# Attention of the first batch in float32 in a cross-attention and FFN kernel, with its inputs on two queues and a new order

## The chip, the cores and the metric

The kernel runs on one core of a Trainium2 chip. The measure is device time in microseconds (us) of the slowest core, here the only one. Three runs of the kernel before took 427.7, 428.87 and 428.94 us; the median is 428.87.

The core has five engines that run side by side, each through its own list of instructions in order: TensorE (PE; the loading of its weights is shown apart, as PEld), VectorE (DVE), ScalarE (ACT), GpSimd (POOL) and SyncE (SP), which here does nothing but start transfers. Engines wait for each other by semaphores.

## The reference

The input `x` is 8 batches x 512 tokens x 512 columns, `ctx` 8 x 64 memory tokens x 512, and a mask says which memory tokens count. First comes attention over the memory tokens, then a feed-forward network (FFN) whose weights are rounded to three values and whose activations are rounded to 8 bits:

```python
def _L0_xattn_ref(hidden_states, memory_tokens, memory_mask):
    scale = 1.0 / jnp.sqrt(D)
    scores = jnp.einsum('bsd,bmd->bsm', hidden_states, memory_tokens) * scale
    scores = jnp.where(memory_mask[:, None, :], scores, -1e30)
    attn = jax.nn.softmax(scores, axis=-1)
    readout = jnp.einsum('bsm,bmd->bsd', attn, memory_tokens)
    valid_b = jnp.any(memory_mask, axis=-1)
    return jnp.where(valid_b[:, None, None], readout, 0)

def _rmsnorm(x, g):
    return g * (x * jax.lax.rsqrt(jnp.mean(x * x, axis=-1, keepdims=True) + EPS))

def _act_quant(x):
    scale = 127.0 / jnp.clip(jnp.max(jnp.abs(x), axis=-1, keepdims=True), 0.0001, None)
    return jnp.clip(jnp.round(x * scale), -128, 127) / scale

def _ternary_quant(w):
    s = jnp.mean(jnp.abs(w))
    return jnp.round(jnp.tanh(w / (s + EPS))) * jnp.arctanh(s)

def _linear_bit(x, w, g):
    return jnp.einsum('bsd,od->bso', _act_quant(_rmsnorm(x, g)), _ternary_quant(w))

x = x + _L0_xattn_ref(_layernorm(x), ctx, mask)
y = _layernorm(x)
h = _silu(_linear_bit(y, w1, g1)) * _linear_bit(y, w2, g2)
x = x + _linear_bit(h, w3, g3)
```

`w1` and `w2` are 2048 x 512, `w3` is 512 x 2048, all float32 (4 MB each). Before a weight can be rounded, the mean of all its magnitudes must be known, so all of it must have been read.

## The kernel before, in words

**The program and its order.** The kernel first records its program as a list of operations in a `Plan`: each has an engine, an estimated cost for the planner, the call that issues it, and the buffers that it reads and writes. Some have several `ways` (the same work on another engine). `ORDER`, a compressed string, holds the order in which all operations are issued and the way that each takes; it was written by a planner outside the program. `Plan.order` decodes it, gives each tile its place in its pool, and the program is issued in just that order:

```python
    order, ways = plan.order()
    with tc.manual_schedule():
        for o in order:
            plan.ops[o].ways[ways[o]][2]()
```

So each engine's list is fixed, and so is that of SP, which starts every transfer of the program: all inputs, all outputs and all transposes that a DMA makes (`Q` is SP). `A` is ACT, `V` DVE, `G` POOL, `T` PE. The cost numbers in the calls of `op` do not reach the chip.

**Tiles.** A batch is four tiles of 128 tokens (tile c of batch b; partition p holds tokens 4p to 4p+3). The 64 memory tokens of a batch lie twice, in partitions 0 to 63 and 64 to 127, in `mem_b`, loaded by two transfers of 128 KB (`load_x`, L469 to 487). `both_b` holds two batches' memory tokens for `measure_mem` (L489 to 526), which finds the power of two of each batch's largest magnitude and from it the scales `f`. Batch 0's x comes in two halves of 512 KB, other batches' in one of 1 MB.

**Attention.** It is done with float16 pairs: a float32 value is written as a high half (a cast to float16) plus a low half (the rest, cast again), and both go through float16 products.
- `split_mem` (L528) makes `ms`, the scaled memory tokens as a pair (high half on ACT L533, low half on DVE L536), and their transpose `mT`.
- `pre` (L542): statistics of x by DVE (L560, L562), the normalised tile `t` (L582, L586), its pair `xh` (L591, L592), its transpose `xT`, and scores `psc` (L602), eight products of 128x128 with k over the four 128-column blocks of both halves. Then two passes on DVE put scale, bias of the mask and the second half of the scores together (L614, L618), the maximum (L622) and the difference (L624).
- `expo` (L630): the exponential, on ACT (L645).
- `post` (L651): the sum and its inverse, times the scale in `f` (L663), the pair `ph` of the weights (high half, and L670 for the low half), its transpose `pT`, the readout `po` (L683, eight products of 128x512), and x plus the readout (L691).
- `flip` (L293 to 310) transposes a float16 tile: for batch 0 on PE, with a copy from PSUM to SBUF by DVE (L309) or ACT (L310); for other batches by a transpose in a DMA that SP starts.

Batch 0 goes through this in two halves, tiles 0 and 1, then 2 and 3. `masks` (L274 to 287) loads the mask (64 KB), and DVE makes `keep`, the bias and `valid` (which batches have any token) from it.

**The weights.** `load_w` (L316) reads each weight in four quarters, `raw_i_k`, of 1 MB. `measure_w` (L339 to 373) sums the magnitudes of each quarter, on ACT (L353) or DVE (L354), the last quarter in two halves; one product with a matrix of constants adds the partitions (`pm`, L363), and DVE makes the mean and the scale `ws` (L371). `quantise_w` (L380) then rounds each quarter: it scales to a float16 that rounds by its own spacing (`tq`, on POOL L386 or ACT L387, or DVE), transposes it on PE (`pw`, 16 transposes, L396) and clips it into `w1T`, `w2T` or `w3T` on DVE (L390 by its line). `arctanh` makes the factor `alpha`.

**The FFN.** `quantise_x` makes z for one or two tiles: the second layernorm (`xm`, L721, L725, L731), times g1 and g2 (`z`, L736 on POOL), the largest magnitude (L741), the rounding (L799, L800) and the transpose `zT`, on PE for batch 0 and by DMA for batches 1 to 7. For each tile, `gate` and `up` make `p` by `linear` (L883; a group is eight products of 128x512, four groups a tile), silu on ACT (L899), the product with it on DVE (`combine`, L927), squares on ACT (L932), g3 (`gain`, L940, on POOL or DVE), the largest magnitude (L964 by its line) and the rounding of h (L997 by ACT, or POOL); two transfers of a transpose make the halves of `hT` (L1002). `down_quarter` multiplies with `w3T` (`pd`, L825), four quarters of four products between the groups of a later tile, and DVE adds to x (L835). The last tile of all has its own order (`down_last`, L854).

During the FFN of batch b, the attention of batches b+1 and b+2 and the z of batch b+1 are worked on between the groups (`during`). For batch 0, the rounding of w3 stands there too. PSUM has three places of two banks that `p`, `pw`, `po` and the transposes of batch 0 share.

## Time and profile before

One execution was profiled. It took 427.9 us in all; the span of its instructions, from the first to the last, is 425.8 us.

| | busy us | share of the span | instructions |
|---|---|---|---|
| PE, products | 388.8 | 91% | 2174 |
| DVE | 369.0 | 87% | 832 |
| ACT | 341.3 | 80% | 464 |
| POOL | 368.7 | 87% | 330 |
| DMA, mean of the span | 67.35 MB at 158 GB/s | | |

The costliest groups of instructions:

| line, engine, work | count | busy us | mean ns of one |
|---|---|---|---|
| L883 PE, p from w1 | 512 | 120.4 | 383 |
| L883 PE, p from w2 | 512 | 119.2 | 379 |
| L825 PE, pd | 496 | 117.8 | 379 |
| L940 POOL, h times g3 | 55 | 130.4 | 2377 |
| L927 DVE, combine | 64 | 81.9 | 1280 |
| L964 DVE, largest of h, 2048 columns | 31 | 70.6 | 2278 |
| L899 ACT, silu | 64 | 70.1 | 1105 |
| L592 POOL, low half of x | 32 | 37.3 | 1168 |

A product's shown 380 ns is longer than the time by which the next follows it (16 products of 512 columns stand in the chain of waits with 3.46 us: 216 ns for one, 1.73 us for a group of eight), since products overlap.

Busy time is the union of an engine's instructions. In the views that follow, the slices cut the span in 40 equal parts of 10.6 us and give the busy share in tenths (9 is 90% or more); PEclk is the clock that TensorE was granted, in tenths. The chain of waits follows back from the last instruction to what released each; its lines give start, length and what ran. The timeline gives start, length, engine, line and operation, and in brackets how long the engine had been idle and for what.

Up to 40 us the transfers moved 13.87 MB, 347 GB/s in the mean. The mask (64 KB) landed 3.2 us after its issue, a half of batch 0's x 6.1 us, a `both` 8.7 us, a quarter of a weight 13.8 us (medians of the first 40 us). ACT's first instruction, the load of a table of 1.28 us, is followed by its first copy of memory tokens; it was idle 8.5 us for that. DVE's reduction of batch 0's `both` took 0.69 us.

### The profile page before, as it was taken

To read this page: it belongs to the slowest core of one execution; us is meant where nothing else is said; L and a number is where in the kernel's file an instruction comes from. 1 tells how busy PE (TensorE), PEld (TensorE's weight loads), DVE (VectorE), ACT (ScalarE), POOL (GpSimd) and SP (SyncE) were. 2 spreads that over 40 slices of the span, in tenths; PEclk is the share of its full clock that TensorE was granted. 3 is DMA by queue.
4 is the path that set the end of the run, shared out by engine and by line. 5 is a ranking of instruction groups with operands and counts; after the bars stand their busy time and mean duration, and the time that the engine had idled before them with its cause. 6 is when DMAs were issued, how large, how long until landed. Compare 5 with 4: busy or idle time off the path is not lost.

```text
span 425.8 us, 6677 instructions
## 1 busy us (share of the span) xinstructions
PE 388.8 (91%) x2174; PEld 192.8 (45%) x2174; DVE 369.0 (87%) x832; ACT 341.3 (80%) x464; POOL 368.7 (87%) x330
## 2 busy tenths in 40 slices
PE   0563878999999999999999999999999999999996
PEld 0341534544444544454445444544454444444444
DVE  4689999999998998799989998999789888897772
ACT  1799999979899799598996898988686986774531
POOL 1789998998999999699999999999699979988650
PEclk9996899999999999999999999999999999999999
DMA  7999994497555578863589635864644546533272
GB/s 217 408 406 376 380 208 52 103 255 147 126 112 150 99 131 157 183 174 68 104 158 276 136 76 82 171 174 83 134 76 148 75 87 146 152 77 73 49 207 90
DMA packets 142514, 67.35 MB, mean 158 GB/s; under 512 B 133136, under 2 KB 133520, under 8 KB 140048
## 3 DMA queue, kind: packets, MB, share of 16 engines
q1 hardware_dynamic: 142480, 66.93, 63.4%
q8 instruction: 17, 0.28, 0.3%
q14 instruction: 17, 0.14, 0.1%
HBM read 25.76 MB, written 8.39 MB: 80 GB/s over the span
## 4 chain that ended last, share of the span: by engine, by line
PE 78%; DVE 6%; POOL 6%; DMA 3%; issue 3%; ACT 2%; SPq 0%; DVEq 0%; POOLq 0%; ACTq 0%
PE p L883 48%; PE pd L825 24%; PE po L683 3%; DMA zT<-xm 2%; PE psc L602 2%; POOL tq L386 2%; DVE st L560 1%; DMA both<-in_ctx_dram 1%; PE pd L854 1%; POOL t L586 1%; POOL xh L592 1%; POOL mv L291 1%; DVE zf L741 1%; DVE h L927 1%; ACT h L899 1%
## 5 line engine op out<-in xcount | busy, mean ns | idle before, releaser
L883 PEld LDWEIGHTS <-zT 128*128 128x128 f16 x1024 | 99.5, 98 | 122.0 <-issue 3.0
L940 POOL TENSOR_TENSOR h<-h,g_bc 128x1024 f32<-128x1024 f32 x55 | 130.4, 2377 | 2.7 <-ACT sq L932 2.1
L883 PE MATMUL p<-w1T,zT 128*128 128x512 f16 x512 | 120.4, 383 | 2.4 <-DVE zT L309 1.5
L883 PE MATMUL p<-w2T,zT 128*128 128x512 f16 x512 | 119.2, 379 | 1.1 <-DVE h L927 0.9
L825 PE MATMUL pd<-w3T,hT 128*128 128x512 f16 x496 | 117.8, 379 | 0.0
L927 DVE SCALAR_TENSOR_TENSOR h<-p,zf,h 128x1024 f32<-128x1024 f32 x64 | 81.9, 1280 | 14.9 <-PE p L883 8.4
L899 ACT ACTIVATE h<-p,zf 128x1024 f32<-128x1024 f32 x64 | 70.1, 1105 | 24.8 <-PE p L883 17.0
L932 ACT ACTIVATE sq<-h 128x1024 f16<-128x1024 f32 x64 | 67.2, 1050 | 17.0 <-DVE h L927 14.8
L825 PEld LDWEIGHTS <-hT 128*128 128x128 f16 x496 | 47.9, 98 | 55.6 <-DMA hT<-h 0.2
L964 DVE TENSOR_REDUCE hf<-h 128x1 f32<-128x2048 f32 x31 | 70.6, 2278 | 1.8 <-POOL h L940 1.7
L736 POOL TENSOR_TENSOR z<-xm,g_bc 128x1024 f32<-128x1024 f32 x29 | 69.8, 2423 | 1.4 <-ACT xm L725 0.6
L997 ACT ACTIVATE h<-h,hf 128x2048 f16<-128x2048 f32 x23 | 45.8, 1994 | 0.2 <-DVE hf L968 0.2
L741 DVE TENSOR_REDUCE zf<-z 128x2 f32<-128x1024 f32 x32 | 38.8, 1211 | 5.8 <-POOL z L736 5.7
L592 POOL TENSOR_TENSOR xh<-t,xh 128x512 f16<-128x512 f32 x32 | 37.3, 1168 | 2.0 <-DVE xh L591 1.2
L799 ACT ACTIVATE xm<-z,zf 128x512 f16<-128x512 f32 x42 | 28.1, 709 | 0.7 <-DVE zf L760 0.7
L731 ACT ACTIVATE xsq<-x,xf 128x512 f32<-128x512 f32 x32 | 22.9, 715 | 6.5 <-DVE x L691 6.0
L835 DVE SCALAR_TENSOR_TENSOR x<-pd,hf,x 128x512 f32<-128x512 f32 x31 | 23.1, 744 | 3.0 <-PE pd L825 2.6
L691 DVE SCALAR_TENSOR_TENSOR x<-po,mx,x 128x512 f32<-128x512 f32 x32 | 22.9, 745 | 1.3 <-PE po L683 1.2
L602 PE MATMUL psc<-mT,xT 128*128 128x128 f16 x256 | 19.7, 224 | 1.9 <-DMA xT<-xh 1.9
L560 DVE BATCH_NORM_STATS2 st<-x 128x6 f32<-128x512 f32 x32 | 21.3, 679 | 0.0
L602 PEld LDWEIGHTS <-xT 128*128 128x128 f16 x256 | 16.9, 101 | 8.5 <-DMA xT<-xh 3.5
L291 POOL TENSOR_TENSOR hf<-hf,neg_half 128x1 f32<-128x1 f32 x32 | 20.1, 634 | 0.2
(134 smaller groups left out, 483.4 us busy)
## 6 DMA issues: line engine op xcount, KB each, us to landing
raw<-in_L_ffn_w_dram SPq DMA_DIRECT2D x10, 1024.0 KB, 13.8
x<-in_x_dram SPq DMA_DIRECT2D x7, 1024.0 KB, 6.9
out_dram<-x SPq DMA_DIRECT2D x7, 1024.0 KB, 4.1
mem<-in_ctx_dram SPq DMA_DIRECT2D x16, 128.0 KB, 6.5
w3T<-in_L_ffn_w_dram SPq DMA_DIRECT2D x2, 1024.0 KB, 12.6
both<-in_ctx_dram SPq DMA_DIRECT2D x4, 256.0 KB, 8.2
x<-in_x_dram SPq DMA_DIRECT2D x2, 512.0 KB, 6.1
g_bc<-in_L_ffn_g_dram SPq DMA_DIRECT2D x1, 1024.0 KB, 14.9
```

The lines of the kernel that those rows point to most:

```text
L592: rest = lambda e, t=t, xh=xh: e.tensor_tensor(xh()[:, 1, :], t(), xh()[:, 0, :], ALU.subtract)
L602: T.matmul(psc()[:, c, :, :].rearrange("p s m -> p (s m)"), xT()[:, k, :], mT().rearrange("p (s d) m -> p d s m", s=2)[:, k % ND, :, :], s ...
L736: gain = lambda e, xm=xm, z=z: e.tensor_tensor(z(), xm().broadcast_to([P, 2, D]), g_bc(), ALU.mult)
L741: lambda i=i, z=z, am=am: V.tensor_reduce(am()[:, i, :], z(), AX.X, ALU.max, apply_absolute_value=True),
L825: T.matmul(po(), hT()[:, n * P : (n + 1) * P], w3T()[:, n, :], start=(n == 0), stop=(n == NH - 1),)
L883: T.matmul(ps()[:, k * HC : (k + 1) * HC], zT()[:, g * ND + d, :], weight(d, j * HW // HC + k), start=(d == 0), stop=(d == ND - 1),)
L899: lambda: A.activation(h()[:, j * HW : (j + 1) * HW], ps(), AF.Silu, scale=fac()[:, 0:1]),
L927: lambda: V.scalar_tensor_tensor(cols(), ps(), fac()[:, 1:2], cols(), ALU.mult, ALU.mult),
L932: lambda: A.activation(sq(), cols(), AF.Square, scale=(RMS / H) ** 0.5, accum_out=col(j)),
L940: run = lambda e: e.tensor_tensor(cols(), cols(), g3_bc()[:, j * HW : (j + 1) * HW], ALU.mult)
L964: lambda: V.tensor_reduce(col(2), h(), AX.X, ALU.max, apply_absolute_value=True),
L997: op(ACT, 1995, lambda: A.activation(hq(), h(), AF.Copy, scale=col(5)), [h], [(f, 5)], other=[(POOL, 1970, lambda: G.tensor_scalar(hq(), h ...
```

## The change

- For the batches in `FLOAT`, here batch 0 alone, no pair is made. `turn_float` transposes the float32 tile on PE with the float32 identity, into a PSUM tile of float32, and copies it to SBUF on DVE or ACT; the buffers `mT`, `xT` and `pT` keep their places and are read as float32 by `as_float`. The scores are four float32 products of 128x64 for a tile in place of eight of 128x128 in float16, the readout one of 128x512 for a tile in place of two. One pass on DVE adds the bias, with the constant scale D^-0.5; the inverse of the sum is multiplied by `valid`; the readout is made with `mem` itself.
- The mask and `mem_0` go through ACT's queue, and the memory tokens of each batch come twice into their tile by one transfer with a broadcast source, not by two transfers. (`both_0` is still loaded, since batch 1 needs it.)
- `ORDER` is another. In it SP starts with the first half of x, then `both_0`, the second half of x, and w1's quarters 3, 1, 0, 2. DVE sums the magnitudes of two and a half quarters of w1 in place of ACT, DVE multiplies more tiles by g3, and the copies of batch 0's transposes are on ACT.
- A few costs for the planner change; they do not reach the chip.

```diff
--- before.py
+++ after.py
@@ -149,47 +150,47 @@
 
 
 ORDER = """
...
 """
 BIG, XM, BOTH = 9, 2, 1
 LAST = 1
+FLOAT = (0,)
 TURNED = ((0, 1, 2, 3), (0, 1, 2, 3), (0, 1, 2, 3))
 Z_TURNED = (0, 1, 2, 3)
 AHEAD = 0
@@ -272,8 +273,8 @@
         op(DVE, 140, lambda: V.tensor_copy(ident_h(), ident()), [ident_h], [ident])
 
     def masks():
-        op(DMA, (475, 650, 200, 500),
-           lambda: Q.dma_start(
+        op(DMA, (60, 650, 200, 500),
+           lambda: A.dma_start(
                mask_u8().rearrange("p b m -> p (b m)"),
                mask.rearrange("b m -> (b m)").partition_broadcast(P)),
            [mask_u8], [])
...
@@ -467,16 +468,18 @@
     xs, mts, att_state, mem_f = {}, {}, {}, {}
 
     def load_x(b):
-        if b % 2 == 0:
+        if b % 2 == 0 and not {b, b + 1} <= {*FLOAT}:
             both = plan.buffer(att, "both", [P, D], F32, BOTH, f"both_{b}")
             op(DMA, (475, 650, 729),
                lambda: Q.dma_start(both(), mem[b : b + 2].rearrange("b m d -> (b m) d")), [both], [])
             mem_f[b] = mem_f[b + 1] = measure_mem(b, both)
         mt = plan.buffer(att, "mem", [P, D], F32, 2, f"mem_{b}")
-        for half in range(2):
-            op(DMA, (475, 650, 364, 500),
-               lambda half=half: Q.dma_start(mt()[half * M : (half + 1) * M, :], mem[b]),
-               [(mt, half)], [])
+        queue = A if b == 0 else Q
+
+        op(DMA, (60 if b == 0 else 475, 650, 700, 500),
+           lambda: queue.dma_start(
+               mt(), mem[b : b + 1].broadcast_to([2, M, D])),
+           [(mt, 0), (mt, 1)], [])
         xt = plan.buffer(big, "big", [P, NC, D], F32, BIG, f"x_{b}")
         view = x[b].rearrange("(p c) d -> p c d", c=NC)
         n = 2 if b == 0 else NC
@@ -485,6 +488,10 @@
                lambda c=c: Q.dma_start(xt()[:, c : c + n, :], view[:, c : c + n, :]),
                [(xt, c + i) for i in range(n)], [])
         mts[b], xs[b] = mt, xt
+
+    def as_float(buf, n):
+
+        return buf().rearrange("p n r -> p (n r)").bitcast(F32).rearrange("p (n r) -> p n r", n=n)
 
     def measure_mem(b, both):
 
@@ -525,7 +532,24 @@
            [(f, 3)], [pe, valid])
         return f
 
+    def turn_float(name, buf, made, rows, n, src, reads):
+
+        pt = plan.buffer(ps_mm, "mm", [P, n, rows], F32, 3, f"pt_{name}")
+
+        def turn():
+            for i in range(n):
+                T.transpose(pt()[:, i, :], src()[:, i * P : (i + 1) * P], ident()[:rows, :rows])
+
+        op(PE4, 107 * n * rows // P, turn, [pt], [*reads, ident])
+        op(DVE, 151 + n * rows * 25 // 24, lambda: V.tensor_copy(made(), pt()), [buf], [pt],
+           other=[(ACT, 140 + n * rows * 5 // 6, lambda: A.copy(made(), pt()))])
+
     def split_mem(b):
+        if b in FLOAT:
+            mT = plan.buffer(att, "mT", [P, 2 * ND, M], F16, 2, f"mT_{b}")
+            turn_float(f"m_{b}", mT, lambda: as_float(mT, ND), M, ND, lambda: mts[b]()[0:M, :],
+                       [(mts[b], 0)])
+            return mts[b], mT, None
         mt, f = mts[b], mem_f[b]
         ms = plan.buffer(att, "ms", [P, 2, D], F16, 2, f"ms_{b}")
         mT = plan.buffer(att, "mT", [P, 2 * ND, M], F16, 2, f"mT_{b}")
@@ -586,6 +610,20 @@
                        lambda c=c, t=t, scale=scale, shift=shift, by=by: by.tensor_scalar(
                            t(), xt()[:, c, :], scale(), shift(), ALU.mult, ALU.add))
                       for e, by, cost in ((POOL, G, 762), (DVE2, V, 545))])
+            if b in FLOAT:
+                xT = plan.buffer(att, "xT", [P, 2 * ND, P], F16, 2, f"xT_{b}_{c}")
+                turn_float(f"x_{b}_{c}", xT, lambda xT=xT: as_float(xT, ND), P, ND, t, [t])
+
+                def score(c=c, xT=xT):
+                    for k in range(ND):
+                        T.matmul(
+                            psc()[:, c, 0, :], as_float(xT, ND)[:, k, :], as_float(mT, ND)[:, k, :],
+                            start=(k == 0), stop=(k == ND - 1),
+                        )
+
+                op(PE4, 860, score, [(psc, c)], [xT, mT])
+                yield
+                continue
             xh = plan.buffer(att, "xh", [P, 2, D], F16, 2, f"xh_{b}_{c}")
             op(ACT, 612, lambda t=t, xh=xh: A.copy(xh()[:, 0, :], t()), [(xh, 0)], [t],
                other=[(DVE2, 413, lambda t=t, xh=xh: V.tensor_copy(xh()[:, 0, :], t()))])
@@ -610,14 +648,17 @@
             yield
         bias_b = lambda: mask_bias()[:, b : b + 1, :].broadcast_to([P, n, M])
         part, cost = lambda: sc()[:, lo:hi, :], 139 + 67 * n
+        by = (lambda: float(D) ** -0.5) if b in FLOAT else (lambda: f()[:, 3 + b % 2 : 4 + b % 2])
+        scaled = [] if b in FLOAT else [(f, 2)]
         op(DVE, cost + 66,
            lambda: V.scalar_tensor_tensor(
-               part(), psc()[:, lo:hi, 0, :], f()[:, 3 + b % 2 : 4 + b % 2], bias_b(), ALU.mult, ALU.add),
-           [(sc, lo)], [*((psc, c) for c in tiles), (f, 2), mask_bias])
-        op(DVE, cost + 66,
-           lambda: V.scalar_tensor_tensor(
-               part(), psc()[:, lo:hi, 1, :], f()[:, 3 + b % 2 : 4 + b % 2], part(), ALU.mult, ALU.add),
-           [(sc, lo)], [*((psc, c) for c in tiles), (f, 2)])
+               part(), psc()[:, lo:hi, 0, :], by(), bias_b(), ALU.mult, ALU.add),
+           [(sc, lo)], [*((psc, c) for c in tiles), *scaled, mask_bias])
+        if b not in FLOAT:
+            op(DVE, cost + 66,
+               lambda: V.scalar_tensor_tensor(
+                   part(), psc()[:, lo:hi, 1, :], by(), part(), ALU.mult, ALU.add),
+               [(sc, lo)], [*((psc, c) for c in tiles), *scaled])
         top = lambda: mx()[:, lo:hi]
         op(DVE, cost, lambda: V.tensor_reduce(top(), part(), AX.X, ALU.max),
            [(mx, lo)], [(sc, lo)])
@@ -635,7 +676,7 @@
             for b in batches:
                 post_state[b] = (
                     plan.buffer(att, "pr", [P, NC, M], F32, 1, f"pr_{b}"),
-                    plan.buffer(att, "ph", [P, NC, 2, M], F16, 1, f"ph_{b}"),
+                    None if b in FLOAT else plan.buffer(att, "ph", [P, NC, 2, M], F16, 1, f"ph_{b}"),
                     plan.buffer(att, "pT", [P, NC, P], F16, 1, f"pT_{b}"),
                 )
                 x_sum[b] = few("xf", NC, b)
@@ -659,33 +700,47 @@
         op(DVE, 139 + 67 * n, lambda: V.tensor_reduce(rs(), part(), AX.X, ALU.add),
            [share], [(pr, lo)])
         op(DVE, 163, lambda: V.reciprocal(rs(), rs()), [share], [])
+        keep, kept = (valid, valid) if b in FLOAT else (f, (f, 3))
+        at_b = b if b in FLOAT else 5 + b % 2
         by_column(
             lambda e, at, n: e.tensor_scalar(
-                rs()[:, at : at + n], rs()[:, at : at + n], f()[:, 5 + b % 2 : 6 + b % 2], 1.0,
+                rs()[:, at : at + n], rs()[:, at : at + n], keep()[:, at_b : at_b + 1], 1.0,
                 ALU.mult, ALU.mult),
-            n, [share], [(f, 3)])
-        high, low = (lambda k=k: ph()[:, lo:hi, k, :] for k in range(2))
-        op(ACT, 190 + 54 * n, lambda: A.copy(high(), part()), [(ph, (lo, 0))], [(pr, lo)],
-           other=[(DVE2, 139 + 34 * n, lambda: V.tensor_copy(high(), part()))])
-        rest = lambda e: e.tensor_tensor(low(), part(), high(), ALU.subtract)
-        op(POOL, 100 + 143 * n, lambda: rest(G), [(ph, (lo, 1))], [(pr, lo), (ph, (lo, 0))],
-           other=[(DVE2, 139 + 67 * n, lambda: rest(V))])
-        flip((pT, lo), [(ph, (lo, 0)), (ph, (lo, 1))], lambda: pT()[:, lo:hi, :],
-             lambda: ph()[:, lo:hi, :, :].rearrange("p c s m -> p (c s m)"), n, P, f"p_{b}_{lo}",
-             b == 0)
+            n, [share], [kept])
+        if b in FLOAT:
+
+            turn_float(f"p_{b}_{lo}", (pT, lo), lambda: as_float(pT, NC // 2)[:, lo // 2 : hi // 2, :],
+                       P, n // 2, lambda: part().rearrange("p c m -> p (c m)"), [(pr, lo)])
+        else:
+            high, low = (lambda k=k: ph()[:, lo:hi, k, :] for k in range(2))
+            op(ACT, 190 + 54 * n, lambda: A.copy(high(), part()), [(ph, (lo, 0))], [(pr, lo)],
+               other=[(DVE2, 139 + 34 * n, lambda: V.tensor_copy(high(), part()))])
+            rest = lambda e: e.tensor_tensor(low(), part(), high(), ALU.subtract)
+            op(POOL, 100 + 143 * n, lambda: rest(G), [(ph, (lo, 1))], [(pr, lo), (ph, (lo, 0))],
+               other=[(DVE2, 139 + 67 * n, lambda: rest(V))])
+            flip((pT, lo), [(ph, (lo, 0)), (ph, (lo, 1))], lambda: pT()[:, lo:hi, :],
+                 lambda: ph()[:, lo:hi, :, :].rearrange("p c s m -> p (c s m)"), n, P, f"p_{b}_{lo}",
+                 b == 0)
         yield
         for c in range(lo, hi, 2):
             po = plan.buffer(ps_mm, "mm", [P, 2, D], F32, 3, f"po_{b}_{c}")
 
             def read(c=c, po=po):
                 for i in range(2):
+                    if b in FLOAT:
+                        half = slice(i * M, (i + 1) * M)
+                        T.matmul(
+                            po()[:, i, :], as_float(pT, NC // 2)[half, c // 2, :], ms()[half, :],
+                            start=True, stop=True,
+                        )
+                        continue
                     for s in range(2):
                         T.matmul(
                             po()[:, i, :], pT()[:, c + i, :], ms()[:, s, :],
                             start=(s == 0), stop=(s == 1),
                         )
 
-            op(PE, 864, read, [po], [(pT, lo), ms])
+            op(*(PE4, 1706) if b in FLOAT else (PE, 864), read, [po], [(pT, lo), ms])
             for i in range(2):
                 op(DVE, 753,
                    lambda c=c, i=i, po=po: V.scalar_tensor_tensor(
...
```

## The prediction

> **What bounds the kernel now.** The page first: the engines' busy line and the slices. Then the windows, the chain of waits from 20 to 83 us, the timeline around its turning points, and TensorE's own waits after 76 us.
>
> ```profile
> PE   0563878999999999999999999999999999999996
> ...
> PEclk9996899999999999999999999999999999999999
> ```
> ```profile
> 10.00:20.00 10.00, 4.92 (x44) 3.71 (x44) 6.18 (x17) 7.74 (x9) 7.05 (x10) 1.00 1.05 408
> ...
> 50.00:60.00 10.00, 8.53 (x72) 4.99 (x71) 9.87 (x27) 10.00 (x15) 9.30 (x13) 1.00 1.19 243
> ...
> 110.00:140.00 30.00, 30.00 (x153) 14.16 (x152) 27.57 (x84) 28.30 (x42) 29.27 (x29) 1.00 0.50 120
> ```
> ```profile
> PE p L883 <- DMA zT<-xm: 1.1, 2, 0.9
> PE p L883 <- DVE h L927: 0.4, 1, 0.4
> ```
>
> The window columns are PE, weight loads, DVE, ACT, POOL (busy, count), clock, DMA share, GB/s. From 80 us to the end TensorE is full, and its waits after 76 us come to 1.5 us. So the end is set by two things: when TensorE becomes full, and whether it stays so. Before that, from about 20 us on, DVE, ACT and POOL are all near full and TensorE is not; before 20 us nothing is full but the DMA engines (share 1.05).
>
> ```profile
> 24.89 1.97 POOL tq L386
> ...
> 62.38 1.76 ACT tq L387
> 69.64 1.13 DVE w3T L390
> ...
> 83.01 1.19 PE pd L825 x5
> ```
> ```profile
> 20.12 1.06 ACT L353 ACTIVATE w2T<-raw 128x1024 f16<-128x1024 f32 x1 [0.52 <-DMA raw<-in_L_ffn_w_dram]
> ...
> 24.19 0.16 DVE L371 RECIPROCAL ws<-ws 128x1 f32<-128x1 f32 x1
> ...
> 71.28 1.99 ACT L387 ACTIVATE tq<-raw,ws 128x2048 f16<-128x2048 f32 x1
> ...
> 79.28 1.23 DVE L390 TENSOR_SCALAR w3T<-pw 128x2048 f16<-128x2048 f16 x1
> ...
> 82.94 1.90 PE L825 MATMUL pd<-w3T,hT 128*128 128x512 f16 x8
> ```
>
> I read three marks. The last quarter of w1 lands at 20.1 us; w1's scale ws is ready at 24.35 (24.19 + 0.16), and the rounding of weights begins (24.89). ACT rounds its last quarter of w3 until 73.27, DVE clips the last one by 80.5. The first down product pd starts at 82.94, and TensorE is full from there. In the two programs' orders 11 gate or up groups of eight 512-column products stand ahead of that first pd, in both; behind it the same 936 remain. So the change is worth what it moves this mark, plus what TensorE waits after it.
>
> **The arithmetic of batch 0.** Removed: POOL 4 low halves xh (4 x 1.16) and 2 ph (2 x 0.43), 5.5 us; DVE 4 casts (4 x 0.38), ms (0.75), 2 second score passes (2 x 0.35), ph (0.22), 3.2 us; ACT ms and ph, 1.0 us. Moved from DVE to ACT: the four xT copies, 0.69 each on DVE; on ACT I take 0.585 each (the 128x512 mT row), at most 1.0 (the 128x1024 zT row). Most of this lies between 10 and 23 us, where the three engines were busy 6.2, 7.7 and 7.1 of 10 us and w1 had not landed: there it is worth nothing by itself. It counts as room for DVE to take 2.5 quarters of w1's magnitudes (2 x 2.28 by the 2048-column reduction, 1.21 by the 1024-column one, 5.8 us); ACT loses 1.06 + 2 x 1.91 = 4.9 us there.
>
> **The float32 products.** A float32 transpose of 128 columns shows 0.27 us (0.37 once) alone, against 0.61 for eight in float16; a float32 product shows as two records, 0.34 to 0.55 for the pair. So 16 transposes cost 0.9 (float16 pitch, 0.056) to 4.4 us, 16 score products 0.9 to 5.4, and the four 512-column po 0.9 (0.216 each) to 4.2 (0.27/0.056 as dear). In their place 44 + 32 short (76 x 0.056 = 4.3) and 8 long float16 products (1.7) go, 6.0 us. TensorE is busy 4.9, 6.0 and 4.0 of 10 us there, so I count 0; on the path of one tile it is 4 x 0.27 instead of 0.61, half a microsecond. If the cover were gone, at most 4.4 + 5.4 + 4.2 - 6.0 = 8.0 us; DVE's sum row of the first tiles stands behind the reduction of w1's second quarter, which lands near 15 us, so at least one microsecond of lateness is free. The clock granted at 30 to 50 us (0.81, 0.68) can stretch the second po, late next: x of tiles 2 and 3, 0.9 us of cover by DVE's work.
>
> The Trainium skill, "FP8 and Floating Point Precision", section "TensorE Precision Notes", says that true float32 takes four passes through the array, which speaks against the change. By it po would be 4 x 4 x 0.216 = 3.5 us, inside the bounds above; no row here shows a long float32 product.
>
> **Transfers.** SP issued mask, both, mem and x in 0.40 to 0.59 us each and the first w1 quarter at 4.00; now two x and one both stand ahead of it, so about 2.4. Mask (64 KB) and mem (256 KB) go through ACT, whose queue has only its table load (1.28) and batch 0's first copy behind them; DVE's keep and, through it, the first statistics wait for the mask, landing by 4.5 (3.2 after issue at about 1.3). The bytes ahead of w1's end are the same, and 0 to 10 us moved 204 GB/s against 408 after, so w1 may land 0 to 1 us sooner: bounds 19.1 to 20.1, maybe 20.3 if the small packets are slower together. I take 20.0, nearest to the row. What is later in SP's queue is used after 35 us. In the queue, hT's second half now stands behind pT of batch 1, whose low half ph DVE makes after its last clip; it would land near 85, when TensorE is at its second pd quarter: 0, at worst 1 us.
>
> The skill, "DMA: Bandwidth & Descriptors", section "Issuing engines are not separate DMA queues", says the queues share the 16 DMA engines and a second issuer saves only issue time. By it the second queue is worth 0 to 1.6 us at the issue and 0 at the last byte; the 408 GB/s row agrees.
>
> **The path, summed.** w1's last quarter 20.0; ACT 1.9; product, mean and scale: 0.7 (23.17 to 23.88) and 0.5, so ws at 23.1, 1.2 sooner. DVE's reduction of the third quarter ends by 21.3 (lands near 17.4), its sum row by 22.3: no bound. From there I add each engine's instructions in program order with the durations above, to the mark before the first pd:
> - ACT, from w1's magnitudes to its last w3 quarter: 50.5 us of instructions before, which took 50.1 on the clock (23.17 to 73.27); 53.1 now, so 52.6, from 22.0: 74.6.
> - DVE, from ws to its last w3 clip: 61.3 before in 56.2 us (short ones overlap); 59.7 now, so 54.7, from 23.1: 77.8, if nothing it needs is late.
> - POOL, to hT's rounding: 49.8 before in 54.1 us; 49.6 now, 53.9 from 23.4: 77.3, and 2.8 for its transfer, 80.1.
> Behind ACT's 74.6: 0 to 1.1 for a PSUM place (its silu), 1.07 transposes, two groups 3.46, the small float32 pair 0.31: TensorE is at the first pd at 79.4 to 80.5; the two clips left (2.9) end by 79.7. I take 80.2, 2.7 us before 82.94.
>
> After it the order is new. By the same addition POOL has 32 us less in the whole program, DVE 2 and ACT 3 more; the work ahead of each batch's zT on DVE is like before's. 1.5 us of waits stood there; I take 0.5 more, bounds -1 and +6.3 (below). At the end 48 pd products (10.4 us) cover the last tile's chain, about 9.5; no change. Sum: span 425.8 - 2.7 + 0.5 = 423.6; the execution lies 2.1 outside its span (427.9), so 425.7. The runs shown are 427.7 to 428.94 with this profile among the low ones, so I add 0.5: **426.2**.
>
> **The rivals.** The first, where ACT takes the gain: its list is longer by 2.6 us; were its float32 copies 1.0 instead of 0.585 (4 x 0.42 = 1.7) and ws no sooner (1.2), pd stands at 83.1 and the time is no change, 428.9. For it: ACT was 10.00 of 10 at 50 us. Against: it idled from 14 to 20 us waiting for weights. The second, slower: TensorE waits for zT at the start of batches 1 to 7, since SP's in-order queue holds other transposes ahead of them. One such wait was 0.9; seven make 6.3, in place of my 0.5: 432.0. It decides from 0.65 us a batch. For it: two waits before, both of this kind. Against: POOL, which makes z, has more room. The third, that float32 is not the gain, but w1 lands at 19.1 and ACT's 2.3 us of idle before 73 vanish: 423.0.
>
> **Chances.** Mine 0.52 (its own range 424 to 428), no change by ACT 0.20, zT waits 0.18, the larger gain 0.10. About 0.3% (1.3 us) is what can be told from no change. Faster: the larger gain and nearly all of mine, 0.60; same 0.20, slower 0.20. The range takes in the first and third rivals and the lower part of the second: 422.6 to 430.4.
>
> **What would show it.** ws at about 23.1; ACT's last w3 quarter at 74.6; first pd at 80.2, with TensorE's waits after it under 2.5 us. A first pd at 83 or waits for zT over 4 us make it wrong; a float32 po over 4 us, with DVE idle before x, would show my cover gone.

## The result, and the profile after

The changed kernel took 462.38 us in the median of four runs (461.27 to 463.21), the kernel before 428.88 beside it: a ratio of 1.0787, 95% interval 1.0757 to 1.0816. I had forecast 426.2, and my range ended at 430.4.

The profiled execution took 463.21 us with a span of 461.4. The slices, as before (span in 40 equal parts, now of 11.5 us):

```profile
PE   0387584997996988997999989999999999999996
...
PEclk9999787999898999999999999999999999999999
```

TensorE starts later, and has holes up to the middle of the span that the kernel before has not. The marks I had read, in the timeline after (L541 is the new float32 transpose, L372 the scale of a weight, L388 and L391 its rounding and clip, L880 the down product):

```profile
15.08 0.66 PE L541 MATMUL pt_m<-ident,mem 64*128 64x64 f32 x4 [15.08 <-DMA mem<-in_ctx_dram]
15.73 0.43 DVE L282 CAST keep<-mask_u 128x512 f32<-128x512 uint8 x1 [15.73 <-DMA mask_u<-in_mask_BxS_bk_dram]
...
35.03 0.16 DVE L372 RECIPROCAL ws<-ws 128x1 f32<-128x1 f32 x1
...
89.74 1.99 ACT L388 ACTIVATE tq<-raw,ws 128x2048 f16<-128x2048 f32 x1
...
96.91 1.20 DVE L391 TENSOR_SCALAR w3T<-pw 128x2048 f16<-128x2048 f16 x1
...
99.23 0.60 PE L880 MATMUL pd<-w3T,hT 128*128 128x512 f16 x2
```

The memory tokens and the mask, first in ACT's queue, are there at 15.1 and 15.7 us; DVE's first instruction waits for the mask. w1's scale is ready at 35.2 us (before 24.35, forecast 23.1), the first down product stands at 99.2 (before 82.94, forecast 80.2): 16.3 us lost there. The other half is behind it. TensorE's waits from 99 us on (in total, times, longest):

```profile
PE p L938 <- DMA zT<-xm: 6.5, 3, 3.8
PE pd L880 <- DMA hT<-h: 3.0, 1, 3.0
PE psc L640 <- DMA xT<-xh: 2.9, 2, 2.5
PE p L938 <- DVE zf L804: 1.2, 1, 1.2
PE p L938 <- ACT h L954: 1.0, 1, 1.0
```

With two smaller ones 15.8 us, of which 15.5 come from the first down product on, where the kernel before has 1.1; 12.4 are waits for transposes made by a DMA. One of these, in the chain of waits and in SP's timeline (L480 loads memory tokens, L299 and L1057 are transposes):

```profile
137.82 8.76 DMA zT<-xm
```
```profile
136.96 0.57 SPq L480 DMA_DIRECT2D mem<-in_ctx_dram  x1
137.82 4.22 SPq L299 DMA_TRANSPOSE zT<-xm  x1
...
146.62 0.85 PE L938 MATMUL p<-w1T,zT 128*128 128x512 f16 x2 [3.84 <-DMA zT<-xm]
```

A transpose of zT lands in 3.2 us in the median. This one took 8.76, and it stands right behind a load of memory tokens. What the DMA engines did meanwhile, in the windows (last columns: clock, share of the 16 DMA engines, GB/s) and in the DMA view of 140 to 145 us:

```profile
140.00:145.00 5.00, 2.78 (x13) 1.08 (x11) 4.80 (x11) 4.60 (x7) 5.00 (x8) 1.00 0.13 50
```
```profile
DMA packets 122, 0.25 MB, mean 50 GB/s; under 512 B 0, under 2 KB 0, under 8 KB 122
```

Only packets of 2 KB move, the rows of memory tokens; the share is 0.13, two engines of sixteen, and 50 GB/s is an eighth of the 408 that full engines moved. So the new transfer, one of 128 rows with a broadcast source, runs on two engines. At 50 GB/s its 256 KB take 5.2 us alone, and everything queued behind it on those two engines waits, although fourteen are idle.

The mask at the start shows the same. It stands behind `mem_0` in ACT's queue and moves in 128 packets of 512 B. By the DMA view, 112 of these (seven eighths, as fourteen engines of sixteen would carry) move from 4 to 9 us, none from 9 to 13.8, and the last 16 from 13.8 to 15.4, when the memory tokens are through.

### The profile page after: what moved, and what is told of

Read it like the earlier page. It is cut to its first block, busy times and chain, and to the rows that moved or that the text cites. A ratio compares the mean times of both kernels' runs of the same rounds, so it can differ in the third digit from the quotient of the medians.

```text
span 461.4 us, 6587 instructions
## 1 busy us (share of the span) xinstructions
PE 403.8 (88%) x2152; PEld 203.4 (44%) x2152; DVE 378.7 (82%) x760; ACT 344.3 (75%) x470; POOL 346.7 (75%) x344
## 2 busy tenths in 40 slices
DMA packets 142274, 67.35 MB, mean 146 GB/s; under 512 B 132896, under 2 KB 133280, under 8 KB 139808
## 4 chain that ended last, share of the span: by engine, by line
PE 44%; POOL 9%; DVE 6%; DMA 6%; issue 3%; ACT 2%; SPq 0%; DVEq 0%; POOLq 0%; ACTq 0%
PE p L938 26%; PE pd L880 15%; POOL h L995 3%; DMA hT<-h 3%; POOL z L791 2%; DMA zT<-xm 2%; PE po L738 1%; DVE zf L796 1%; POOL xh L630 1%; DMA xT<-xh 1%; DVE ms L560 1%; DVE h L982 1%; PE psc L640 1%; PE pd L909 1%; DVE z L791 1%
## 5 line engine op out<-in xcount | busy, mean ns | idle before, releaser
L938 PEld LDWEIGHTS <-zT 128*128 128x128 f16 x1024 | 100.7, 99 | 132.6 <-issue 12.5
L938 PE MATMUL p<-w1T,zT 128*128 128x512 f16 x512 | 124.5, 390 | 8.3 <-DMA zT<-xm 6.5
L995 POOL TENSOR_TENSOR h<-h,g_bc 128x1024 f32<-128x1024 f32 x50 | 119.9, 2403 | 12.8 <-ACT sq L987 12.4
L880 PE MATMUL pd<-w3T,hT 128*128 128x512 f16 x496 | 120.1, 380 | 4.1 <-DMA hT<-h 3.0
L954 ACT ACTIVATE h<-p,zf 128x1024 f32<-128x1024 f32 x64 | 70.6, 1107 | 29.7 <-PE p L938 11.0
L987 ACT ACTIVATE sq<-h 128x1024 f16<-128x1024 f32 x64 | 67.2, 1050 | 14.8 <-DVE h L982 14.4
L880 PEld LDWEIGHTS <-hT 128*128 128x128 f16 x496 | 47.9, 98 | 60.7 <-DMA hT<-h 4.7
L791 POOL TENSOR_TENSOR z<-xm,g_bc 128x1024 f32<-128x1024 f32 x23 | 57.9, 2526 | 5.0 <-ACT xm L780 4.0
L1052 ACT ACTIVATE h<-h,hf 128x2048 f16<-128x2048 f32 x24 | 47.9, 1995 | 6.2 <-DVE hf L1023 6.2
L630 POOL TENSOR_TENSOR xh<-t,xh 128x512 f16<-128x512 f32 x24 | 28.0, 1172 | 9.3 <-ACT xh L628 9.2
L584 DVE BATCH_NORM_STATS2 st<-x 128x6 f32<-128x512 f32 x32 | 21.3, 677 | 5.6 <-DMA x<-in_x_dram 5.6
L640 PE MATMUL psc<-mT,xT 128*128 128x128 f16 x224 | 18.3, 229 | 8.4 <-DMA mT<-ms 5.5
L995 DVE TENSOR_TENSOR h<-h,g_bc 128x1024 f32<-128x1024 f32 x14 | 19.2, 1376 | 6.0 <-ACT sq L987 6.0
L628 ACT CAST xh<-t 128x512 f16<-128x512 f32 x25 | 15.1, 610 | 11.0 <-DMA xT<-xh 10.9
## 6 DMA issues: line engine op xcount, KB each, us to landing
raw<-in_L_ffn_w_dram SPq DMA_DIRECT2D x10, 1024.0 KB, 15.8
```

The lines of the kernel that those rows point to most:

```text
L630: rest = lambda e, t=t, xh=xh: e.tensor_tensor(xh()[:, 1, :], t(), xh()[:, 0, :], ALU.subtract)
L791: gain = lambda e, xm=xm, z=z: e.tensor_tensor(z(), xm().broadcast_to([P, 2, D]), g_bc(), ALU.mult)
L880: T.matmul(po(), hT()[:, n * P : (n + 1) * P], w3T()[:, n, :], start=(n == 0), stop=(n == NH - 1),)
L938: T.matmul(ps()[:, k * HC : (k + 1) * HC], zT()[:, g * ND + d, :], weight(d, j * HW // HC + k), start=(d == 0), stop=(d == ND - 1),)
L954: lambda: A.activation(h()[:, j * HW : (j + 1) * HW], ps(), AF.Silu, scale=fac()[:, 0:1]),
L987: lambda: A.activation(sq(), cols(), AF.Square, scale=(RMS / H) ** 0.5, accum_out=col(j)),
```

## The experiments

I first did not see this. I took the second queue to be the cause (theory A below), with the broadcast read as a rival (theory C), and changed one part at a time. ws (w1's scale, at the end of its last operation) and the first down product (pd) are from the profiles; "waits" is TensorE's waiting after its first down product. Each ratio is to runs of the kernel before on the same chip (medians of 427.9 to 429.5).

| run | time | ratio to before, 95% | mask used | ws ready | first pd | waits |
|---|---|---|---|---|---|---|
| kernel before | 428.88 | | 3.95 | 24.4 | 82.9 | 1.1 |
| changed kernel | 462.38 | 1.0757 to 1.0816 | 15.73 | 35.2 | 99.2 | 15.5 |
| e1_sp | 460.23 | 1.0712 to 1.0780 | 10.00 | 29.5 | 96.4 | 15.7 |
| e4_w1_act | 458.76, one run | | 16.06 | 35.5 | 97.1 | 14.0 |
| e4b_halves | 434.41, one run | | 9.59 | 29.0 | 85.5 | 4.5 |
| e6_bcast_later | 454.03, one run | | 9.01 | 28.5 | 92.1 | 14.5 |
| e7_before_bcast | 464.0, one run | | 4.81 | 29.7 | 99.0 | 15.5 |
| e2_before_act | 431.13 | 1.0039 to 1.0080 | 6.05 | 27.4 | 86.1 | 1.0 |
| e12_before_x_first | 432.04 | 1.0057 to 1.0086 | 9.31 | 28.0 | 86.7 | 1.4 |
| e5_halves_sp | 431.0 | 1.0051 to 1.0108 | 6.30 | 27.3 | 84.2 | 1.8 |
| e10_quarter_score | 429.95, one run | | 6.35 | 24.6 | 82.0 | 3.6 |
| e9_scale_first | 433.2 | 1.0081 to 1.0117 | 6.38 | 24.2 | 87.1 | 1.9 |
| e11_scores_sooner | 429.36 | 0.9995 to 1.0027 | 6.23 | 24.9 | 81.3 | 2.0 |
| e13_mask_x_mem | 427.6 | 0.9939 to 0.9982 | 4.47 | 23.4 | 80.5 | 3.8 |

**The queue or the transfer.** e1_sp:

```diff
-           lambda: A.dma_start(mask_u8() ...
+           lambda: Q.dma_start(mask_u8() ...
-        queue = A if b == 0 else Q
+        queue = Q
```

> The changed kernel, with the mask and mem_0 issued by SP, ahead of x, both and w1, in place of ACT; all else is kept. Theory A (the two transfers on ACT's queue got only a share of the DMA engines beside w1 on SP's queue, so they landed at 15.1 and 15.7 us; everything after is that lateness passed on): DVE starts on the mask before 5 us, ws is ready at 24 to 26 instead of 35.2, the first down product stands at 81 to 86 instead of 99.2, TensorE's waits after it fall under 5 us from some 16, and the time is 426 to 434. Theory B (the start cost 11 us and no more; the new order itself, with its waits for DMA transposes, costs the rest): the first down product is about 11 us sooner, at 88, the waits after it stay near 16 us, and the time is 448 to 453. Theory C (the queue is not the cause, the broadcast read of mem_0 is slow): the mask, which now stands behind it in one queue, is still late, and the time stays above 458.

460.23: theory A falls, and the late mask and the time are those of theory C. In one queue, and ahead of everything, mem_0 still landed at 9.9 and the mask, one place behind it, at 10.0; the waits after the first down product stayed.

e4_w1_act puts w1's quarters into ACT's queue too, behind `mem_0` and the mask:

```diff
-                Q.dma_start(t().rearrange("p (j d) -> p j d", d=D), ...
+                (A if i == 0 else Q).dma_start(t().rearrange("p (j d) -> p j d", d=D), ...
```

> The changed kernel, with w1's four quarters also on ACT's queue, behind mem_0 and the mask; x and both stay on SP. Theory A (a queue is served in its order, and the two queues share the engines): mem_0 and the mask land before 7 us since no weight stands in the other queue, and DVE's first instruction starts by 7 us instead of 15.7; x, both may land later than 4 us instead, sharing with w1. Theory C (ACT's queue or the broadcast is slow in itself): they still land after 12 us. The time is under 450 by A, above 455 by C.

`mem_0` and the mask landed at 16.0 and 16.1 us, and the time was 458.76: against A again. One quarter of w2 was still issued on SP, at 2.15 us, so the other queue was not free of weights; e1_sp is the stronger test.

e4b_halves keeps ACT's queue and changes the form of the transfer alone:

```diff
-           lambda: queue.dma_start(mt(), mem[b : b + 1].broadcast_to([2, M, D])),
+           lambda: [queue.dma_start(mt()[h * M : (h + 1) * M, :], mem[b]) for h in range(2)],
```

> The changed kernel, with each batch's memory tokens by two transfers of 128 KB in place of the broadcast one; mem_0 and the mask stay on ACT's queue. Theory A: no difference, mem_0 and the mask land at 14 to 16 us and the time is 458 to 466. Theory C (the broadcast form is what is slow): they land before 8 us and the time falls under 450.

434.41: 28 us of the loss of 33.5 are gone with this line, as theory C said. mem_0 landed at 6.7 us, but the mask, behind it in the queue, only at 9.59, later than the 8 us that I gave both. Two lines of the pages' queue part (packets, MB, share of 16 engines) show the form; first the changed kernel, then e4b_halves:

```profile
q10 hardware_dynamic: 274, 0.33, 0.2%
```
```profile
q10 hardware_dynamic: 304, 0.33, 0.3%
```

This is ACT's queue, with mem_0 and the mask. The bytes are the same, and the two halves have 30 packets more. A half of 64 rows that ends on 16 engines with one small packet each makes 80, so two make 160; 128 rows that end on two engines make 130. The trace holds these small packets, of 4 bytes: 18 in the first of the two queues and 48 in the second, where the mask, on 16 engines, has 16 in both. So 2 and 32 are left for `mem_0`. The difference of 30 is there eight times in the whole program (142514 packets against 142274). I call this theory D: a broadcast transfer is carried by two engines, and what is queued behind it on them waits.

e6_bcast_later has two halves for mem_0 and the broadcast for the other seven:

```diff
+           lambda: [queue.dma_start(mt()[h * M : (h + 1) * M, :], mem[b]) for h in range(2)]
+           if b == 0 else queue.dma_start(mt(), mem[b : b + 1].broadcast_to([2, M, D])),
```

> The changed kernel with two transfers of 128 KB for mem_0 alone, still on ACT's queue; mem_1 to mem_7 keep the broadcast one. It parts the loss of 28 us (462.4 against 434.4 with no broadcast) into that of the start and that of the later batches. Theory D: both count. The start is then as without any broadcast (first down product near 86 to 92, since mem_1 and mem_2 lie ahead of it), TensorE's waits after it stay near 12 to 16 us, and the time is 446 to 455. Theory E (only the first, landing at 15 us, counts, the rest is slack): 434 to 438.

454.03, as D said: the first broadcast transfer costs about 8 us (462.4 - 454.0), the seven later ones some 20 (454.0 - 434.4), with the waits for transposes. Both are differences to single runs.

e7_before_bcast puts the broadcast alone into the kernel before:

```diff
-               lambda half=half: Q.dma_start(mt()[half * M : (half + 1) * M, :], mem[b]),
+               lambda half=half: half or Q.dma_start(mt(), mem[b : b + 1].broadcast_to([2, M, D])),
```

> The kernel before, its order, pairs and queue kept, with one broadcast transfer in place of the two of each batch, at the place of the first. Theory D: this one part of the change makes it slower by itself, by 10 to 30 us (439 to 459), with waits for transposes after the first down product. Theory G (the broadcast hurts only in the new order, which leaves transposes less room): under 435.

464.0, more than I gave it: this one line makes the kernel before as slow as the whole change does. Its waits from 99 us on are all for transposes:

```profile
PE pd L826 <- DMA hT<-h: 5.9, 2, 3.1
PE p L884 <- DMA zT<-xm: 5.3, 1, 5.3
PE psc L603 <- DMA xT<-xh: 4.3, 1, 4.3
```

So the broadcast transfer is shown to be the loss in both orders, taken out of the new one and put into the old one: 28 and 36 us, where the runs of any one kernel here lie within 4.5 us. That it does this by being two engines wide rests on the packets and on the share of 0.13.

**The other parts of the transfers, each alone in the kernel before.** e2_before_act:

```diff
-           lambda: Q.dma_start(mask_u8() ...
+           lambda: A.dma_start(mask_u8() ...
-               lambda half=half: Q.dma_start(mt() ...
+               lambda half=half: (A if b == 0 else Q).dma_start(mt() ...
```

> The kernel before, with its own order, float16 pairs and half transfers, where the mask and the two halves of mem_0 are issued by ACT in place of SP; nothing else is changed. Theory A: the mask lands after 12 us instead of 3.9, ws comes 8 to 12 us later than 24.35, and the time is 437 to 455, so that one part of the change alone makes it slower. Theory B: some 11 us lost, 438 to 442. Theory C (broadcast): within 3 us of 428.9.

431.13, 0.4 to 0.8% slower: with its halves the second queue costs some 2 us (429.14 beside it), not 10. The mask came at 6.05 instead of 3.95, and with it the first of DVE's instructions that waits.

e12_before_x_first issues x's first half, both_0, x's second half, the mask and the halves of mem_0 in this order:

```diff
     order, ways = plan.order()
+    ahead = [21, 9, 22, 5, 20, 19]
+    order = ahead + [o for o in order if o not in ahead]
```

> The kernel before with its six first transfers in another order on SP, nothing else: the first half of x, both_0, the second half of x, the mask, and the two halves of mem_0; then w1 as it was. This is the part of the change that puts the first tokens first, alone. My forecast counted it at 0, since w1's landing at 20.1 and its magnitudes set ws, not x: ws at 24.0 to 25.0 and 427.5 to 430.5. A rival: x is what the first statistics wait for, so DVE, which starts on the mask, gains: ws or the first down product over 0.8 us sooner and a time under 427.5. The other: the mask, now at 2.1 us in the queue, holds DVE's first instruction to 5.5 or later and the time is above 430.5.

432.04: slower by 0.6 to 0.9%. The mask, of 64 KB behind 1.25 MB, came at 9.31, and it is what DVE's list waits for first; ws came at 28.0. The second of the rivals that I wrote held. mem_0, also moved back, came at 10.9 instead of 8.5, but ACT's first copy of it then waited until 12.81 for a scale from DVE, so the mask was the later of the two.

**What is left of the change without the broadcast.** e5_halves_sp joins the edits of e1_sp and e4b_halves.

> The changed kernel with two edits: every batch's memory tokens by two transfers of 128 KB in place of the broadcast one, and the mask and mem_0 issued by SP ahead of x. Theory D (a broadcast transfer is carried by 2 of the 16 DMA engines: 130 packets against 160 for two halves, and a DMA share of 0.13 with 49 to 53 GB/s where it runs alone at 140 to 145 us of the changed kernel; whatever is queued behind it on these two waits, transposes too): with that gone, what is left against the kernel before is the queue and the rest of the change. If ACT's queue is worth the 2 us that it cost in the kernel before, this is 432; if mask and mem_0 first in one queue bring DVE's start to under 5 us, ws comes at about 24 and the first down product at 80 to 83, as I forecast for the whole change, and the time is 425 to 430. Theory F (the float32 products, now on the path of the first tiles, cost what the pairs saved): ws at 26 or later, first down product at 84 or later, 431 to 436.

431.0, ws at 27.3 and the first down product at 84.2: theory F's numbers. TensorE's float32 groups in its first 40 us, by shape (count, busy us, mean ns), and what stood in DVE's list:

```profile
L618 PE MATMUL psc<-mT,xT 128*128 128x64 f32 x32 | 7.6, 426 | 2.0 <-ACT xT L544 2.0
L540 PE MATMUL pt_x<-ident,t 128*128 128x128 f32 x16 | 3.9, 424 | 0.0
L731 PE MATMUL po<-mem,pT 64*128 64x512 f32 x8 | 3.2, 886 | 0.1
```
```profile
22.05 0.29 DVE L653 SCALAR_TENSOR_TENSOR sc<-psc,mask_bias 128x128 f32<-128x128 f32 x1 [2.96 <-PE psc L618]
22.37 0.28 DVE L662 TENSOR_REDUCE mx<-sc 128x2 f32<-128x128 f32 x1
23.51 0.29 DVE L699 TENSOR_REDUCE mx<-pr 128x2 f32<-128x128 f32 x1 [0.86 <-ACT pr L685]
23.72 2.28 DVE L358 TENSOR_REDUCE part<-raw 128x1 f32<-128x2048 f32 x1
```

The last line is the third of DVE's sums of w1, and the scale waits for it. It stands behind two passes on scores that wait for TensorE.

e10_quarter_score leaves out three of four blocks of batch 0's scores:

```diff
-                    for k in range(ND):
+                    for k in range(1):
...
-                            start=(k == 0), stop=(k == ND - 1),
+                            start=True, stop=True,
```

> The kernel of two half transfers with mask and mem_0 on SP, where batch 0's scores use one of the four 128-column blocks (12 of 16 float32 products of 128x64 are left out, 5.5 us of TensorE by 3.68 us for eight of them): its output is not the reference's. Theory F (the float32 scores are on the path that sets ws): DVE's first score pass, at 22.05 before, starts at 19 to 20 and ws at 24 to 25 instead of 27.2, the first down product 0.5 to 2.5 us sooner. If they are covered, ws stays within 0.5 us of 27.2.

DVE's first score pass began at 19.28. ws came at 24.6, 2.8 us sooner, and the first down product 2.2 sooner, so the float32 scores are on that path. But the time, 429.95 in one run, is that of e5's profiled execution (429.95): waits after the first down product, 3.6 us in place of 1.8, took it back, 1.3 us for z's factors at 153 us and 1.0 for a transpose at 98 among them.

e9_scale_first moves w1's last two sums (84, 86), the product, mean, scale and inverse (89 to 92) and the first rounding (93) ahead of the first score pass of tiles 0 and 1 (45):

```diff
     order, ways = plan.order()
+    ahead = [84, 86, 89, 90, 91, 92, 93]
+    order = [o for o in order if o not in ahead]
+    order[order.index(45):order.index(45)] = ahead
```

> The kernel of two half transfers with mask and mem_0 on SP (431.0 us, ws at 27.2, first down product at 84.2), with seven operations issued sooner, ahead of batch 0's first scores on DVE: the magnitudes of w1's quarters 0 (DVE) and 2 (ACT), the product, mean, scale and inverse behind them, and POOL's first rounding of w1. Theory F (w1's scale was late since its last magnitudes stood in DVE's and ACT's lists behind scores that waited for float32 products, not since w1 landed late): DVE sums quarter 0 by 21.5, ACT quarter 2 by 22.3, ws stands at 23 to 24, POOL's first rounding begins by 24.5 instead of 27.7, the first down product comes 1 to 3 us sooner, at 81 to 83.5, and the time is 427.5 to 430. Theory H (w1 itself lands late in this kernel): ws stays at 26 or later, and the time within 1 us of 431.

ws came at 24.2, close to the 23 to 24 expected, and yet the time rose to 433.2, the first down product to 87.1. ACT's sum of the last quarter began at 20.99, as it landed, and DVE then idled 2.47 us for the mean and POOL 7.99 for the scale, with the first score pass behind them. What I had moved back, batch 0's attention, was as urgent as what I had moved forward: TensorE waited 3.9 us before tile 2's scores. Both of my theories missed that.

e11_scores_sooner moves one operation, TensorE's scores of tile 3 (71), behind the first score pass of tiles 0 and 1 (45):

```diff
     order, ways = plan.order()
+    order.remove(71)
+    order.insert(order.index(45) + 1, 71)
```

> The kernel of two half transfers with mask and mem_0 on SP (431.0 us, ws at 27.2, first down product at 84.2), with one operation moved: the float32 scores of tile 3 are issued behind DVE's first score pass on tiles 0 and 1, not ahead of it. In that kernel the pass waited until 22.05 for TensorE, although the scores of tiles 0 and 1 were done at 18.46; nothing is left out. Theory F (the pass waits for the last write to the score tile that stands ahead of it in the program, and w1's last magnitudes wait behind the pass): the pass starts at 19.1 to 19.4, ws at 24.3 to 25.5, the first down product 1 to 2.5 us sooner. The time: 428.5 to 430.5 if the start decides; within 0.5 us of 431 if the new order's later waits take it back, as where the scores were cut to a quarter (first down product at 82.0, span still 427.9).

```profile
19.03 0.28 DVE L653 SCALAR_TENSOR_TENSOR sc<-psc,mask_bias 128x128 f32<-128x128 f32 x1
```

The pass begins at 19.03 in place of 22.05, with no work left out; ws at 24.9, the first down product at 81.3 (2.9 us sooner, more than I gave it), and 429.36, no different from the kernel before (interval 0.9995 to 1.0027).

e13_mask_x_mem adds an order of the first transfers that serves who waits first, the mask, x's first half, mem_0, both_0, x's second half:

```diff
+    ahead = [5, 20, 19, 9, 21]
+    order = ahead + [o for o in order if o not in ahead]
```

> The last kernel (two half transfers, all on SP, tile 3's scores behind the first score pass; 429.36 us, no change to the kernel before) with SP's first five transfers in the order mask, first half of x, mem_0, both_0, second half of x. It joins what the runs spoke for. The mask then lands near 4 instead of 6.2 and x's first half near 7 instead of 9.0, so batch 0's statistics and scores run 1.5 to 2 us sooner; w1's last quarter, landing at 21.1, bounds the rest. If w1 decides (my reading): ws at 24.0 to 24.8, first down product at 80.5 to 81.5, the time 428 to 429.5, no more than 0.3% from the kernel before. If x's chain still decides: ws under 24, the first down product under 80.3, and 426 to 428, faster than both kernels.

427.6, faster than the kernel before by 0.2 to 0.6%. Its marks are those that I had forecast for the change itself:

```profile
4.47 0.43 DVE L282 CAST keep<-mask_u 128x512 f32<-128x512 uint8 x1 [4.47 <-DMA mask_u<-in_mask_BxS_bk_dram]
...
20.06 1.91 ACT L354 ACTIVATE w2T<-raw 128x2048 f16<-128x2048 f32 x1 [0.98 <-DMA raw<-in_L_ffn_w_dram]
...
23.19 0.16 DVE L372 RECIPROCAL ws<-ws 128x1 f32<-128x1 f32 x1
```

w1's last quarter is summed as it lands, and ws follows at 23.35. So w1 decides, as I read it; but it landed at 20.06 and not at 21.1, and both ws and the time lie below the ranges that I wrote for that case. The profiled execution took 428.71 us, more than the median; the twelve lie between 425.05 and 429.5. What float32 alone is worth stays open: this kernel also has the new `ORDER` and a new order of transfers, and no run has this order of transfers with the pairs.

## Why the prediction was wrong

**What bounds the kernel** was read rightly: without the broadcast the time follows the first down product and TensorE's waits after it. With it a third part comes in: of the 35.6 us of span, 16.3 are the later first pd and 14.4 the waits; of the other 4.9, 3.4 are a lower clock after two of the waits (last section), and 1.5 stay open.

**The step that failed is "Transfers".** I wrote "The bytes ahead of w1's end are the same" and priced the new transfer of memory tokens by its bytes, as if any 256 KB were spread over all engines; the merging of two transfers into one was not costed as an edit of its own at all, nor bounded by a rival. Measured, it is 28 us in the new order (e4b_halves, one run) and about 36 in the old (e7_before_bcast, one run, against 427.94 beside it). The mask, which I had landing by 4.5 us, stood behind the new transfer in ACT's queue and came at 15.7. The price could have been seen in the code: the source has a leading dimension of 2 with no step. The Trainium skill, "DMA: Bandwidth & Descriptors", section "Rules for kernel authors", says that a leading broadcast of c copies confines a DMA to at most c engines. The row of 140 to 145 us agrees: a share of 0.13, 50 GB/s. The same section advises one 128-partition transfer over two to disjoint halves; here the two halves were the faster by 28 us, since the one had the broadcast.

**ACT's queue** I counted as 0 to 1 us of gain, the mask landing by 4.5. Alone it costs 0.4 to 0.8% (e2_before_act), the mask coming at 6.05. **The first tokens first** I counted at 0; alone it costs 0.6 to 0.9% (e12_before_x_first), because DVE's list waits for the mask first. I had named that wait in "Mask (64 KB) and mem (256 KB) go through ACT" but added nothing for what is ahead of the mask on the engines.

**"The float32 products ... I count 0"** failed in size and in cover. Sixteen score products took 7.6 us, above my upper bound of 5.4; transposes of x 3.9 (bound 4.4), po 3.2 (bound 4.2). The cover I named, that DVE's sum of w1 is what the first tiles wait for, was not there: in e5_halves_sp DVE's second sum ended at 19.09, 3.0 us before the first score pass could start, and the last sum stood in DVE's list behind score passes that wait for TensorE, which e10_quarter_score (ws 2.8 us sooner) and e11_scores_sooner (2.4) show. "DVE's reduction of the third quarter ends by 21.3" was 26.0 in e5_halves_sp.

**The path, summed**, was right from ws on: I had 57.1 us from there to the first pd, and it is 57.1 in e13_mask_x_mem, 56.9 in e5_halves_sp and 56.4 in e11_scores_sooner (64.0 in the changed kernel itself). ws at 23.1 was wrong for the change as it stood even without the broadcast, 27.3 in e5_halves_sp; that e13_mask_x_mem has 23.35 and 80.5 is the work of two moves in the order that I had not forecast. **The part after it** I took as 0.5 us more waiting; from the first pd on (0.4 of the 1.5 that I read stands ahead of it) it is 0.7 more in e5_halves_sp and 2.7 in e13_mask_x_mem. There the first pd is 2.5 us sooner and the median only 1.5. "POOL has 32 us less in the whole program, DVE 2 and ACT 3 more" came out as 22 less, 5.5 and 2.1 more in e5_halves_sp (busy time).

**The rivals.** The slower one had the right symptom, waits for transposes in SP's queue, at 0.9 us for each of seven batches; it named as cause other transposes ahead of them. The cause was loads ahead of them, two engines wide, and its price was far larger. No rival held that the change of a transfer's form could itself be the loss.

## What to carry to other kernels

Price a transfer by how it is spread, not by bytes alone: look at its outermost dimension, and in a trace at the share of the DMA engines while it runs alone. When a change of many parts is judged, give each edit a line in the sum, those that look like tidying too. An in-order list is as late as its first waiting instruction: before work is put ahead of a mask, or a product ahead of a pass, look whose list it holds. That a broadcast with the rows as its outermost dimension would be fast was not tried.

## What the runs showed of the hardware

A transfer that occupies two of sixteen engines holds up whatever is behind it and needs all of them: zT's transpose took 8.76 us from issue to landing instead of 3.2, and SP itself was held for 4.22 us in issuing it. The last 16 of the mask's 128 packets came some 5 us behind the others.

Two of TensorE's waits cost more than their length. In the windows of the changed kernel after the waits of 2.52 and 3.84 us (the column ahead of the last two is the granted clock):

```profile
117.00:119.00 2.00, 2.00 (x12) 1.30 (x11) 0.69 (x1) 1.20 (x2) 1.07 (x5) 0.50 0.90 180
146.60:148.60 2.00, 1.98 (x6) 0.76 (x7) 0.28 (x4) 0.00 (x0) 1.28 (x2) 0.56 1.10 219
```

The granted clock is 0.50 from 116.1 to 119.5 us and from 146.9 to 150.3; the eight products from 146.62 stand in the chain with 3.41 us, not 1.73. Half the clock over twice 3.4 us costs at most 3.4 us, of the 4.9 that the later first pd and the waits leave over. In e1_sp the same working leaves 6.8 us beside 13.7 us at half clock, which cost at most 6.8, and in e4b_halves 0.6 us beside none.

After the wait of 3.05 that ended at 213.16 the clock stayed at 1.00, so the length of a wait does not tell it. What the windows show is how busy TensorE was in the 3.41 us ahead of each low stretch: 1.23 us (112.72 to 116.13) and 0.23 (143.44 to 146.85). Counted on in the same steps of 3.41 us, the wait at 213 falls over two of them, with 1.82 and 1.96 us of work. These four steps fit a clock that follows the share of work in a step. They do not give the rule: in e9_scale_first the clock stayed at 1.00 behind two steps with 0.84 and 0.98 us of work (21.68 to 28.51).

A DVE pass that reads the scores of tiles 0 and 1 waited until those of tile 3 were written, a write that came first in the program; with the order of these two operations changed the pass began 3.0 us sooner, and the whole went from 431.0 to 429.36 us. That the reason is the one PSUM tile which all four share is argued, not tested.
